# A TensorE switch around the feed-forward's low-part products, and the third norm's last step on GpSimd, in a one-core decoder layer

## The chip, the cores and the metric

The kernel runs on 1 core of a Trainium2 chip. The metric is the device time of one execution in microseconds (us); the time of a kernel is the median of several runs. Engines are named as in the profile: PE is TensorE's matrix products (PEld its weight loads), DVE is VectorE, ACT is ScalarE, POOL is GpSimd, SP is the engine whose queue issues nearly all DMAs.

## What is computed

One decoder layer over 4 sequences of 1024 tokens with 512 features, float32. Cut to what matters here:

```python
x = layernorm(x + attention(x))                   # 16 features a head, 32 heads
x = layernorm(x + gated_convolution(x, ctx))      # sigmoid, tanh gates, kernel size 2
x = layernorm(x + feed_forward(x))

def feed_forward(x, ternary_weight, bias, act_scale):
    scale = maximum(act_scale, 1e-05)
    x_int = clip(round(x / scale), -127, 127)
    w = ternary_weight.astype(float32) - 1.0      # ternary_weight is drawn from 0, 1, 2
    return einsum('bsi,oi->bso', x_int * scale, w) + bias
```

So the weight of the feed-forward holds only -1, 0 and 1 for these inputs. The kernel does not rely on that: it splits the weight into a part that TensorE's `float32r` format holds (the high part) and the rest (the low part), and multiplies by both.

## The kernel before

The kernel has two halves. `attention` takes about 1700 us of the span. `tail` does the rest twice, once for the batches 0 and 2 and once for 1 and 3, with these stages:

* The second time only: the output projection `project_out` (16 tiles of 128 tokens each for a pair of batches, PE line 292).
* The gate stage: 4 times 2 times 4 gates. One gate is 32 products of 128x171 on PE (line 1205, tiles `pc` then `pa`), four DVE instructions that read them (lines 1209 to 1215) and one activation on ACT (line 1216). `pc` and `pa` have two buffers each, so PE can be two gates ahead of DVE. `combine` (lines 1231 to 1260) finishes a group of 4 gates on POOL, ACT and DVE, with the second norm.
* The feed-forward, `feed_forward`: 16 tiles of 128 tokens. For a tile, `quantise` scales on ACT (line 1281) and clips on POOL, or on DVE for the first tiles (line 1282); `turn` transposes on PE (line 1288, four products) and ACT copies the result to `xq_t` (line 1290); `feed` multiplies on PE (line 1298); `residual` is two DVE instructions (lines 1303 and 1304). The third norm follows in groups of four tiles: mean and variance on DVE (line 1314), a root on ACT (line 138), inversion and shift on DVE (lines 139 and 1321), and last the step `finish` per tile, on ACT where its number is even (line 1332) and on DVE where it is odd (line 142), and a DMA of the tile to the output by SP (line 1337). The very last tile is done in two halves of 256 columns.

`feed` has 8 products for a tile: the four 128-row parts of the high weight `w_hi`, then the four parts of the low weight `w_lo`, all into one PSUM tile:

```python
        for n, w in enumerate((hand.w_hi, hand.w_lo)):
            for f in range(FT):
                last = n == 1 and f == FT - 1
                nc.tensor.matmul(pt, xq_ts[b, t][:, f, :], w[:, f, cols], start=n == f == 0, stop=last)
```

Both weights are made during the first gate stage by `halves_of_w_f`: for each of the four parts a cast (line 255) and a subtraction (line 256) on POOL, and a DMA that writes the difference to DRAM (line 257); last a DMA reads the whole low weight back as `w_lo` (line 261).

The order of the work is written out by hand. `step()` is called after every gate and every tile, and counts; `after(n, work)` runs a piece of work n steps later, so it stands on its engines' queues behind the instructions of that gate or tile. The pieces of `halves_of_w_f` are put at steps 17, 19, 21, 23 and 25 of the first gate stage, which has 32 steps. Each engine executes its own queue in order, and a wait at its head holds everything behind it.

Of the kernel before, what the change touches and what calls it, by code (L numbers as in the profile page):

```python
# [8 lines left out]
F32 = mybir.dt.float32  # L9
F32R = mybir.dt.float32r  # L10
AF = mybir.ActivationFunctionType
ALU = mybir.AluOpType
AX = mybir.AxisListType
PSUM = bass.MemoryType.PSUM

P = 128
B, S, D = 4, 1024, 512
NH, HD = 32, 16
NG = 8
FT = D // P  # L20
# [9 lines left out]
@with_exitstack  # L30
def decoder_kernel(ctx: ExitStack, tc: tile.TileContext, a, out):
    nc = tc.nc

    outer = ctx.enter_context(tc.tile_pool(name="outer", bufs=1))
    ident = outer.tile([P, P], F32, tag="ident", name="ident")
    make_identity(nc, ident)
    eps = outer.tile([P, 1], F32, tag="eps", name="eps")
    nc.gpsimd.memset(eps, EPS)

    dram = ctx.enter_context(tc.tile_pool(name="dram", bufs=1, space=bass.MemoryType.DRAM))
    attn_d = [dram.tile([D, S], F32, tag=f"attn{b}", name=f"attn{b}") for b in range(B)]


    shared = ctx.enter_context(tc.tile_pool(name="shared", bufs=1))
    hand = Handed(tc, a, shared, attn_d, eps)
    with ExitStack() as attn:
        attention(attn, tc, a, attn_d, ident, shared, hand)
    with ExitStack() as rest:  # L50
        tail(rest, tc, a, out, ident, eps, hand, dram)
# [11 lines left out]
class Handed:  # L63
# [74 lines left out]
        nc.scalar.activation(part, mv[:, t0 : t0 + n, 1], AF.Sqrt, bias=self.eps, scale=1.0)  # L138
        return rstd, lambda: nc.vector.reciprocal(part, part)

    def normalised(self, dst, src, mv, rstd, t):
        self.nc.vector.tensor_scalar(
            dst, src, mv[:, t, 0:1], rstd[:, t : t + 1], ALU.subtract, ALU.mult
        )

# [98 lines left out]
        w = self.w_f[:, f, :]  # L244
        self.nc.gpsimd.tensor_scalar_add(w, w.bitcast(mybir.dt.int32), -1.0)

    def halves_of_w_f(self, pool, dram):


        nc, w = self.nc, self.w_f  # L250
        self.w_hi = pool.tile([P, FT, D], F32R, tag="w_hi", name="w_hi")
        low_d = dram.tile([P, FT, D], F32, tag="w_low", name="w_low_d")

        def part(f):
            nc.gpsimd.tensor_copy(self.w_hi[:, f, :], w[:, f, :])
            nc.gpsimd.tensor_sub(w[:, f, :], w[:, f, :], self.w_hi[:, f, :].bitcast(F32))
            nc.sync.dma_start(low_d[:, f, :], w[:, f, :])

        def last():
            self.w_lo = self.shared.tile([P, FT, D], F32R, tag="w_f", name="w_lo")  # L260
            nc.sync.dma_start(self.w_lo.bitcast(F32), low_d)

        return [lambda f=f: part(f) for f in range(FT)] + [last]

    def prepare_rest(self):
        nc = self.nc
# [872 lines left out]
def tail(ctx, tc, a, out, ident, eps, hand, dram):  # L1139
    nc = tc.nc  # L1140
    fir = ctx.enter_context(tc.tile_pool(name="fir", bufs=1))
    bigs = ctx.enter_context(tc.tile_pool(name="bigs", bufs=1))
# [5 lines left out]
    ps_t = ctx.enter_context(tc.tile_pool(name="ps_t", bufs=2, space=PSUM))  # L1148
# [11 lines left out]
    def after(steps, work):  # L1160
        later.append((now + max(steps, 1), work))
# [113 lines left out]
    xqs, xq_ts, stats3 = {}, {}, {}  # L1275
# [16 lines left out]

    def feed(b, t, cols=slice(0, D)):
        pt = ps_o.tile([P, D], F32, tag="o", name=f"pf{b}_{t}_{cols.start}")[:, 0 : cols.stop - cols.start]
        for n, w in enumerate((hand.w_hi, hand.w_lo)):
            for f in range(FT):
                last = n == 1 and f == FT - 1
                nc.tensor.matmul(pt, xq_ts[b, t][:, f, :], w[:, f, cols], start=n == f == 0, stop=last)  # L1298
        return pt

    def residual(b, n, t, pt, cols=slice(0, D), half=0):
# [4 lines left out]
    def third_norm(b, n0, n):  # L1306

        y = ys2[b]
        made = []

        def first():
            for m in range(n0, n0 + n):
                halves = 2 if (b, m) == (B - 1, NT - 1) else 1
                nc.vector.bn_aggr(mv3[b][:, m, :], stats3[b][:, m : m + halves, :].rearrange("p h c -> p (h c)"))
            made.extend(hand.deviations(mv3[b], stat, f"3_{b}", n0, n))

        def invert():
            made[1]()
            shift = stat.tile([P, NT], F32, tag="shift", bufs=4, name=f"shift{b}_{n0}")
            part = slice(n0, n0 + n)  # L1320
            nc.vector.scalar_tensor_tensor(
                shift[:, part], mv3[b][:, part, 0], -1.0, made[0][:, part], ALU.mult, ALU.mult
            )
            made.append(shift)

        def finish(m):
            t = order[m]
            n = 2 if (b, m) == (B - 1, NT - 1) else 1
            for h in range(n):
                part = y[:, t, h * D // n : (h + 1) * D // n]  # L1330
                if m % 2 == 0 or h == 1:
                    nc.scalar.activation(
                        part, part, AF.Identity, bias=made[2][:, m : m + 1], scale=made[0][:, m : m + 1]
                    )
                else:
                    hand.normalised(part, part, mv3[b], made[0], m)
                (nc.scalar if h else nc.sync).dma_start(
                    out[b, t * P : (t + 1) * P, h * D // n : (h + 1) * D // n], part
                )

        return first, invert, [lambda m=m: finish(m) for m in range(n0, n0 + n)]


    order = [t // 2 + t % 2 * 4 for t in range(NT)]
    mv3 = {}

    def feed_forward(batches):
# [6 lines left out]
        for k, (b, n, t) in enumerate(tiles):  # L1354
# [3 lines left out]
            if (b, n) == (B - 1, NT - 1):  # L1358

                for half in range(2):  # L1360
                    cols = slice(half * 256, half * 256 + 256)
                    pt = feed(b, t, cols)
                    residual(b, n, t, pt, cols, half)

                    for work in closing:
                        work()
                    closing = []
            else:
                pt = feed(b, t)
                if k + 3 < len(tiles):  # L1370
                    quantise(tiles[k + 3][0], tiles[k + 3][2], nc.vector if k < 3 else nc.gpsimd)

                while roots:
                    roots.pop()()
                if n >= 6:
                    for work in closing:
                        work()
                    closing = []
                residual(b, n, t, pt)
# [29 lines left out]
    after(5, lambda: hand.load_attention(1, big1))  # L1409
    for m, work in enumerate(scaling):  # L1410
        after(9 + m, work)
    for m, work in enumerate(hand.halves_of_w_f(bigs, dram)):
        after(17 + 2 * m, work)

    k = 0
    for n, batches in enumerate(((0, 2), (1, 3))):
# [11 lines left out]
        for t in range(4):  # L1428
            w = w_next
# [65 lines left out]
```

## Time and profile before

| what | value |
|---|---|
| median of 3 runs (lowest, highest) | 2144.36 us (2143.28, 2148.23) |
| the profiled execution's own time | 2147.72 us |
| its span, first to last instruction | 2145.8 us |
| mean granted TensorE clock | 0.998 |
| PE busy in the span | 2109.5 us (98%) |
| DVE / ACT / POOL busy | 1728.0 / 1388.3 / 977.5 us |
| first feed-forward, first product to the start of the projection | 1854.97 to 1894.92 us |
| second feed-forward, first product to the end of the last | 2099.97 to 2140.12 us |

How to read it: times inside the execution count from the first instruction of the span. A row of the timeline has start, duration, engine, line, operation, output and inputs, shapes and count, and in square brackets the idle time before it with what ended that. An engine that is busy all the time sets the pace of its stage only if the others wait for it. The 1.9 us between the span and the execution's own time lie around the span.

### The profile page before, as it was taken

The numbers are of one execution on the slowest core, as the hardware profiler recorded it, in microseconds if no ns is written. First come the engines' busy times: TensorE is split into PE (matmuls) and PEld (weight loads), VectorE is DVE, ScalarE is ACT, GpSimd is POOL, SyncE is SP. The second block draws the span as 40 slices with busy tenths as digits, with TensorE's granted clock in tenths as the row PEclk, the third lists the DMA queues.
The fourth block names the chain that finished last, engine by engine and source line by source line (L and its number), as shares of the span: only waits on it lengthen the run. The fifth ranks groups of instructions, "written<-read, shape, count | busy, mean of one in ns | idle before, by whom it ended". The sixth has DMA issues, their size and how long they took to land.

```text
span 2145.8 us, 81983 instructions
## 1 busy us (share of the span) xinstructions
PE 2109.5 (98%) x35404; PEld 1528.9 (71%) x35404; DVE 1728.0 (81%) x3068; ACT 1388.3 (65%) x2771; POOL 977.5 (46%) x1298
## 2 busy tenths in 40 slices
PE   9999999999999999999999999999999999999998
PEld 6666666666666666666666666667766799858997
DVE  3678888888888888888888888888897566779667
ACT  1157777777777777777777777777777623521336
POOL 2562534333344334343533333645464369532773
PEclk9999999999999999999999999999999999999999
DMA  7513213332322233122313124422411243270222
GB/s 274 176 52 98 78 50 92 106 123 64 102 54 78 63 103 107 60 88 88 106 54 111 54 75 132 147 64 84 123 47 52 60 163 118 74 279 21 100 78 79
DMA packets 114538, 207.97 MB, mean 97 GB/s; under 512 B 36992, under 2 KB 37248, under 8 KB 114048
## 3 DMA queue, kind: packets, MB, share of 16 engines
q1 hardware_dynamic: 113456, 201.55, 29.4%
q8 instruction: 277, 4.54, 0.9%
q10 hardware_dynamic: 720, 1.18, 0.2%
q14 instruction: 85, 0.70, 0.1%
HBM read 132.41 MB, written 69.73 MB: 94 GB/s over the span
## 4 chain that ended last, share of the span: by engine, by line
PE 84%; DVE 13%; POOL 1%; issue 1%; ACT 1%; DMA 0%; SPq 0%; DVEq 0%; ACTq 0%; POOLq 0%
PE av L872 23%; PE nat L758 15%; PE st L835 10%; DVE mx L771 9%; PE part L60 9%; PE pa L1205 6%; PE pc L1205 6%; PE v L60 5%; PE po L60 3%; PE po L292 3%; PE fold L425 1%; PE proj L60 1%; PE pf L1298 1%; PE fold L60 1%; DVE stats L1304 1%
## 5 line engine op out<-in xcount | busy, mean ns | idle before, releaser
L771 DVE TENSOR_REDUCE mx<-nat 128x1 f32<-128x512 f32 x2048 | 1271.4, 684 | 197.8 <-PE nat L758 179.5
L844 ACT ACTIVATE at<-st 128x512 f32<-128x512 f32 x2016 | 1042.2, 603 | 320.5 <-PE st L835 316.6
L758 PE MATMUL nat<-qk 32*128 32x512 f32 x4096 | 712.1, 421 | 2.2 <-DVE v_sb L658 1.3
L835 PE MATMUL st<-qk 32*128 32x256 f32 x8064 | 681.7, 290 | 0.2
L835 PEld LDWEIGHTS st<-qk 32*128 32x128 f32 x8064 | 526.1, 184 | 4.9 <-issue 2.1
L835 PE MATMUL st<-qk,ones 2*128 2x256 f32 x4032 | 504.1, 287 | 0.0
L872 PE MATMUL av<-at,v_sb 128*32 128x256 f32 x8192 | 499.4, 382 | 4.2 <-ACT at L844 1.3
L758 PEld LDWEIGHTS nat<-qk 32*128 32x128 f32 x4096 | 328.6, 184 | 203.0 <-DVE mx L771 162.6
L872 PEld LDWEIGHTS av<-at,v_sb 128*32 128x32 f32 x8192 | 240.8, 109 | 182.3 <-DVE mx L771 25.2
L835 PEld LDWEIGHTS st<-qk,ones 2*128 2x128 f32 x4032 | 353.6, 183 | 0.0
L1216 ACT ACTIVATE u<-u,b_c 128x512 f32<-128x512 f32 x64 | 46.2, 723 | 159.6 <-DVE u L1215 155.7
L778 POOL CAST neg<-least 128x16 fp32r<-128x16 f32 x64 | 12.7, 199 | 216.0 <-DVE least L776 216.0
L885 DVE TENSOR_TENSOR o_sb<-av,o_sb 128x256 f32<-128x256 f32 x128 | 54.4, 425 | 61.6 <-PE av L872 61.2
L722 POOL TENSOR_TENSOR y<-y,extra 128x256 f32<-128x256 f32 (+8 forms) x152 | 73.5, 518 | 65.9 <-ACT extra L708 65.9
L1212 DVE SCALAR_TENSOR_TENSOR u<-pa,u 128x342 f32<-128x342 f32 x64 | 40.6, 634 | 67.5 <-PE pa L1205 66.3
L921 POOL TENSOR_TENSOR o_n<-o_sb,o_n 128x512 f32<-128x512 f32 x64 | 83.3, 1324 | 13.3 <-DVE u L1213 13.3
L450 POOL TENSOR_TENSOR extra<-extra,highs 128x512 f32<-128x512 f32 x62 | 79.6, 1284 | 5.0
L1205 PE MATMUL pa<-xf,w 128*128 128x171 f32 x512 | 80.4, 308 | 0.5 <-POOL w L196 0.5
L1205 PE MATMUL pc<-xf,w 128*128 128x171 f32 x512 | 79.8, 308 | 0.0
L883 ACT COPY o_sb<-av 128x256 f32<-128x256 f32 x128 | 48.1, 376 | 46.9 <-PE av L872 36.7
L1205 PEld LDWEIGHTS pa<-xf,w 128*128 128x128 f32 x512 | 76.0, 189 | 1.0 <-POOL w L196 1.0
L1205 PEld LDWEIGHTS pc<-xf,w 128*128 128x128 f32 x512 | 76.0, 189 | 0.0
(210 smaller groups left out, 2782.3 us busy)
## 6 DMA issues: line engine op xcount, KB each, us to landing
qk<-qk_d SPq DMA_DIRECT2D x96, 512.0 KB
qk_d<-highs SPq DMA_DIRECT2D x96, 256.0 KB
qk_d<-extra SPq DMA_DIRECT2D x96, 256.0 KB
u<-in_ctx SPq DMA_DIRECT2D x16, 1024.0 KB
xT<-in_xT SPq DMA_DIRECT2D x16, 512.0 KB
o_n<-rec_d SPq DMA_DIRECT2D x128, 64.0 KB
attn<-o_n SPq DMA_DIRECT2D x256, 32.0 KB
y<-in_x SPq DMA_DIRECT2D x16, 512.0 KB
```

The source lines that it names most:

```text
L60: nc.tensor.matmul(pt[r, :], lhsT(f)[:, r], rhs(f), start=f == 0, stop=f == tiles - 1)
L292: nc.tensor.matmul(pt, attn_t[:, f, t * P : (t + 1) * P], self.w_o[:, f, :], start=f == 0, stop=f == FT - 1)
L450: eng.tensor_sub(block, block, high)
L722: eng.tensor_add(c, c, x)
L758: lambda n=n, r=r, turn=turn: nc.tensor.matmul(pts[n], qk_sets[u % 3][turn][r : r + 32, qt * P : (qt + 1) * P], qk_sets[u % 3][2][r : r + ...
L771: nc.vector.tensor_reduce(mxs[u][:, qt, j, kh : kh + 1], pts[n], AX.X, ALU.max, negate=True)
L835: lambda st=st, k=k, n=n, left=left, right=right: nc.tensor.matmul(st[:, k * QW : k * QW + QW], left, right, start=n == 0, stop=n == 2),
L844: nc.scalar.activation(at, st, AF.Exp, scale=0.25)
L872: nc.tensor.matmul(av[32 * j : 32 * j + 32, :], v_sb[b % 2][:, kt, c * VW : c * VW + 32], ats[u, 2 * i + n // 2, j][:, n % 2 * QW : n % 2 ...
L885: nc.vector.tensor_add(o, av, o)
L921: nc.gpsimd.tensor_mul(part, o_sb[:, cols].rearrange("p (s e) -> p e s", e=2), part)
L1205: nc.tensor.matmul(pt, w[i][:, tap, o : o + P], xf[:, tap, i, :], start=i == 0, stop=i == FT - 1)
```

## The change

Three things are changed.

1. In `halves_of_w_f`, two DVE reductions per part take the largest value and the negated smallest value of the low weight. A new piece `compare`, at step 27, reduces these 8 columns to one, multiplies it on PE by a column of positive constants (which adds up the 128 rows), and compares the sum with zero on DVE into a one-word tile `flag`. A new piece `read`, at step 29, loads `flag` into a register of PE.
2. `feed` issues three high products, and then a `Switch` of PE on that register with two arms. Arm 0 has the last high product. Arm 1 has the last high product and the four low ones. There are 33 such places (31 tiles, and one tile in two halves).
3. `finish` of the third norm goes to POOL, but for the last four tiles of batch 3, which stay as they are.

```diff
-    def normalised(self, dst, src, mv, rstd, t):
-        self.nc.vector.tensor_scalar(
+    def normalised(self, dst, src, mv, rstd, t, eng=None):
+        (eng or self.nc.vector).tensor_scalar(
...
+        lows = self.shared.tile([P, 2 * FT + 1], F32, tag="lows", name="lows")
+        flag = self.shared.tile([1, 1], mybir.dt.int32, tag="flag", name="flag")
...
             nc.sync.dma_start(low_d[:, f, :], w[:, f, :])
+            nc.vector.tensor_reduce(lows[:, f : f + 1], w[:, f, :], AX.X, ALU.max)
+            nc.vector.tensor_reduce(lows[:, FT + f : FT + f + 1], w[:, f, :], AX.X, ALU.min, negate=True)
+
+        def compare():
+            top = lows[:, 2 * FT : 2 * FT + 1]
+            nc.vector.tensor_reduce(top, lows[:, 0 : 2 * FT], AX.X, ALU.max)
+            pt = ps.tile([P, FT, P], F32, tag="t", name="any_low")[0:1, 0, 0:1]
+            nc.tensor.matmul(pt, top, self.magic, start=True, stop=True)
+            nc.vector.tensor_scalar(flag, pt, 0.0, None, ALU.is_gt)
+
+        def read():
+            engine = mybir.EngineType.PE
+            why = "a comparison gives nought or one"
+            self.any_low = {
+                engine: nc.values_load(
+                    flag, engines=[engine], min_val=0, max_val=1, skip_runtime_bounds_check_because=why
+                )
+            }
...
-        return [lambda f=f: part(f) for f in range(FT)] + [last]
+        return [lambda f=f: part(f) for f in range(FT)] + [last, compare, read]
...
     def feed(b, t, cols=slice(0, D)):
         pt = ps_o.tile([P, D], F32, tag="o", name=f"pf{b}_{t}_{cols.start}")[:, 0 : cols.stop - cols.start]
-        for n, w in enumerate((hand.w_hi, hand.w_lo)):
-            for f in range(FT):
-                last = n == 1 and f == FT - 1
-                nc.tensor.matmul(pt, xq_ts[b, t][:, f, :], w[:, f, cols], start=n == f == 0, stop=last)
+        def product(w, f, start=False, stop=False):
+            nc.tensor.matmul(pt, xq_ts[b, t][:, f, :], w[:, f, cols], start=start, stop=stop)
+
+        for f in range(FT - 1):
+            product(hand.w_hi, f, start=f == 0)
+        for arm in tc.Switch(hand.any_low, n=2):
+            product(hand.w_hi, FT - 1, stop=arm == 0)
+            if arm:
+                for f in range(FT):
+                    product(hand.w_lo, f, stop=f == FT - 1)
         return pt
...
-                if m % 2 == 0 or h == 1:
+                if b != B - 1 or m < 4:
+                    hand.normalised(part, part, mv3[b], made[0], m, nc.gpsimd)
+                elif m % 2 == 0 or h == 1:
...
-    for m, work in enumerate(hand.halves_of_w_f(bigs, dram)):
+    for m, work in enumerate(hand.halves_of_w_f(bigs, dram, ps_t)):
         after(17 + 2 * m, work)
```

In the order in which the changed program issues its instructions on PE, one `feed` reads: three products; `SwitchStride`; two register instructions; then arm 0, which is a branch prefetch hint, one product and an unconditional branch; then arm 1, which is a hint, five products and an unconditional branch; then the next tile's transposes.

More of the change, by code (lines that the diff above doesn't have):

```diff
@@ L245, in prepare_w_f, with halves_of_w_f @@
         self.nc.gpsimd.tensor_scalar_add(w, w.bitcast(mybir.dt.int32), -1.0)
-    def halves_of_w_f(self, pool, dram):
+    def halves_of_w_f(self, pool, dram, ps):
         nc, w = self.nc, self.w_f
+        lows = self.shared.tile([P, 2 * FT + 1], F32, tag="lows", name="lows")
+        flag = self.shared.tile([1, 1], mybir.dt.int32, tag="flag", name="flag")
         self.w_hi = pool.tile([P, FT, D], F32R, tag="w_hi", name="w_hi")
```

## The prediction

> **What bounds the kernel now.** I read the page's busy times first, then the timeline of PE in a feed-forward, then the DMA queues of the page, because the change adds branches and PE's code comes by DMA.
>
> ```profile
> PE 2109.5 (98%) x35404; PEld 1528.9 (71%) x35404; DVE 1728.0 (81%) x3068; ACT 1388.3 (65%) x2771; POOL 977.5 (46%) x1298
> ...
> q8 instruction: 277, 4.54, 0.9%
> ```
>
> PE is busy 98% of the span, so time that PE loses or saves is lost or saved at the end. The change touches two feed-forwards: PE's first product to the projection's start is 1854.97 to 1894.92 (39.95 us), and the second, to the end of its last product, 2099.97 to 2140.12 (40.15 us). In their steady part one tile looks like this:
>
> ```profile
> 1870.82 0.60 PE L1288 MATMUL tr<-ident,xq 128*128 128x128 f32 x4
> 1871.18 1.16 PE L1298 MATMUL pf<-w_hi,xq_t 128*128 128x512 f32 x4
> 1872.18 1.09 PE L1298 MATMUL pf<-w_lo,xq_t 128*128 128x512 f32 x4
> 1873.11 0.60 PE L1288 MATMUL tr<-ident,xq 128*128 128x128 f32 x4
> ```
>
> From start to start: 0.36 us of transposes, 1.00 of high products, 0.93 of low products, 2.29 a tile, with no idle time. PE sets the pace; the others need less per tile: DVE 0.75 + 0.69 (lines 1303, 1304) + some 0.24 for the means and roots = 1.68 without `finish`, ACT 0.69 + 0.80 + 0.08 = 1.57, POOL 0.62.
>
> **What goes.** The weight is -1, 0 or 1, which the cast of line 255 holds exactly, so the low part and the flag are zero and arm 0 runs: 132 low products, 0.93 us a tile, 30 us of PE in all. If branches were free, the pace would fall to DVE's 1.68.
>
> **What the switch costs.** No row of before shows a computed jump, so I bound it. From below: PE, DVE, ACT and POOL each pass one unconditional branch at the program's start, and in the timeline's first microsecond POOL's instructions before and behind it (0.34 + 0.10 to 0.73) are 0.29 us apart. That is a jump to code that is already there.
>
> From above: a jump to code that isn't. Queue q8 shows how PE's code arrives. Its 277 packets carry 4.54 MB, 16.4 KB each; PE and PEld have 35404 instructions each, 70808 / 277 = 256 a packet. So PE's code is streamed in blocks of 256 instructions, and a packet takes 0.009 x 16 x 2145.8 / 277 = 1.12 us on its DMA engine. Straight code hides this, since a block lasts 2145.8 / 277 = 7.7 us. A jump out of the loaded blocks can't hide it. The nearest row for a whole round trip is the 16 KB transfer of line 793 and the wait of SP's next instruction for its landing:
>
> ```profile
> L793 SPq DMA_DIRECT2D rows_d<-turned x64: 527/542/607, 103.7 to 1660.6; - x64
> ```
>
> ```profile
> SPq L798 <- DMA rows_d<-turned: 80.1, 46, 5.9
> ```
>
> The issue takes 0.54 us, the wait behind it 80.1 / 46 = 1.74. That transfer is cut over many DMA engines, a code block is one packet on one; I add its 1.12. One block fetch F is then estimated at 0.54 + 1.74 + 1.12 = 3.4 us; its ends are 1.12 (the packet alone) and 4.5 (a second packet, of the next block in line, ahead of it).
>
> Are the arms out of the loaded blocks? In the changed program's order a `SwitchStride` stands before the jump: arm n lies n strides behind arm 0. Each arm opens with a prefetch hint for the branch that ends it. I read a hint as a sign that the target is in a block that isn't there yet. Both speak for arms in blocks of their own, with the code behind them in one more. I take this as likeliest. Then the tile's chain on PE's sequencer is: enter the block behind the last switch, whose following block (the next arm 0) is called for now; run about 1.4 us of transposes and three products; wait till F is over; enter the arm, whose hint calls for the block behind; its one product ends at once; wait a second F. A tile takes 2F = 6.8 us in place of 2.29, and PE, DVE, ACT and POOL all fit into it.
>
> * First feed-forward: the first arm has been called for long before; its exit costs F, 15 more tiles 2F each: 31 x 3.4 = 105.4 against 39.95, **+65.5**.
> * Second: 17 switches, and the last tile's result needs no exit: 32 x 3.4 + 0.64 (the last products) = 109.4 against 40.15, **+69.3**.
>
> [...]
>
> **Flag.** The eight reductions of 128x512 are priced at 0.68 each (line 771's row), 1.37 a part, on DVE in the gate stage, which PE paces at 4.67 us a gate. They stand behind POOL's subtraction, and everything DVE owes the next gates stands behind them. The tightest is the first: POOL's subtraction (line 256) starts at 1788.51 and takes 1.28, so the reductions end at 1791.2 and the next `pc` is read by 1791.85. PE needs that buffer at 1792.51: hidden, by 0.65 us.
>
> `compare` is not hidden. PE's product waits for DVE's reduction, and all gates stand behind it. It comes after the 27th gate:
>
> ```profile
> 1828.55 2.50 PE L1205 MATMUL pa<-xf,w 128*128 128x171 f32 x16
> ...
> 1834.04 0.86 DVE L1215 SCALAR_TENSOR_TENSOR u<-pa,u 128x513 f32<-128x513 f32 x1
> ```
>
> PE is done at 1831.05; DVE, late by a clip and two `bn_stats`, ends that gate at 1834.9, and with the small reduction PE goes on at about 1835.2: **+4.2**. An idle PE also loses clock. After 1.89 us of idle at 1721.89 the windows' table has (PEclk is the last column but two):
>
> ```profile
> 1723.00:1727.00 4.00, 4.00 (x18) 4.00 (x17) 1.78 (x4) 0.72 (x1) 2.75 (x3) 0.57 0.98 387
> ```
>
> 0.43 x 4 = 1.7 us lost. I count it twice where PE must be quick again, after `compare` and at the projection: **+3.4** (ends 0 and 3.4). The load of the flag into PE's register lies between 0 (PE's queue still has products) and the 2.3 us of the round trip above; I take **+1**.
>
> **Third norm on POOL.** 28 tiles lose 0.81 us on ACT or 0.53 on DVE. POOL's price is not shown with column operands; between its clip (0.64, line 1282) and a tensor-tensor (1.25, line 1260). I take 0.64, the nearest in form. At 6.8 us a tile it costs nothing; at a pace of 1.7 POOL would need 1.3 to 1.9 a tile, and at 1.9 be the bound. SP's DMAs of the output wait for POOL instead, with the loads of the next stage behind them, which have the projection's 55 us. Batch 3's last four tiles, and so the end of the program, are unchanged.
>
> **Sum.** 65.5 + 69.3 + 4.2 + 3.4 + 1 = 143.4. The profiled execution's 2147.72 becomes 2291.1; against the median, 2144.4 + 143.4 = **2288**.
>
> **Rivals.**
>
> * *One fetch a switch is exposed* (arm 0's block is already there, or the hint comes in time). A tile is F + 1.4 = 4.8: first stage 15 x 4.8 + 3.4 = 75.4 (+35.5), second 16 x 4.8 + 0.64 = 77.4 (+37.3), with the 8.6 of flag and clock +81: 2226. For it: the hint exists. Against: one product after the hint gives it no time.
> * *The code is there* (several blocks loaded ahead, or arms in one block): the other side. The switch is then 0.3 us or less, hidden, and DVE's 1.68 sets the pace: 0.6 us x some 22 steady tiles = 13, less 4.2 + 1.7 + 1 = 6.9 (one clock dip), about -6: 2138, or 2131 if `compare` is hidden too. It decides from 63F + 0.6 + 8.6 = 80.1 on, F = 1.13: a fetch must cost less than a packet alone. For it: nothing in the trace excludes deeper loading. Against: the hints, and one packet per block all along.
> * *F is near its low end of 1.12*: 2.24 a tile is the old pace; no change, 2144.
> * *The flag is not zero* and arm 1 runs: its four low products hide under the fetches; 2288 or a few us above.
>
> **Chances.** Two fetches 0.55, one fetch 0.25, code there 0.13, F small 0.04, flag set 0.03. So faster by over 0.2% 0.13, within 0.2% (about what a measurement of this kernel can tell from no change) 0.04, slower 0.83. Within the likeliest case F from 2.3 (the round trip with no packet added) to 4.5 gives 63 x 2.3 + 0.6 - 80.1 + 8.6 = +74 to +213. The range 2212 to 2350 takes in nearly all of that and the one-fetch case, and leaves out the 17% that end near or below today's time.
>
> **What would show it.** Right: in the feed-forwards PE idles twice a tile with "issue" or nothing as its releaser, tiles 5 to 9 us apart; q8 has two to three more packets per switch, 66 to 99 in all; no `w_lo` products; ACT and DVE wait for PE. Wrong: tiles 1.7 to 2.3 apart with DVE waiting for nothing, q8 near 277, or POOL between PE's tiles.

## The result, and the profile after

The changed kernel takes 2342.53 us (2339.84 to 2343.96) against 2144.94 (2143.28 to 2148.23): 1.0918 times the time before, 95% interval 1.0899 to 1.0937, 197.6 us more. The forecast was 2288 in a range of 2212 to 2350. Its span is 2338.1 us against 2145.8, with a mean granted clock of 0.942 against 0.998.

The page after, the lines that answer to those of before:

```profile
PE 2130.6 (91%) x35274; PEld 1526.1 (65%) x35274; DVE 1723.3 (74%) x3064; ACT 1379.6 (59%) x2757; POOL 1034.8 (44%) x1326
...
PEclk9999999999999999999999999999999955999855
...
q8 instruction: 374, 6.13, 1.2%
...
PE 77%; DVE 12%; issue 6%; POOL 3%; ACT 1%; POOLq 0%; DMA 0%; SPq 0%; DVEq 0%; ACTq 0%
```

PE executes 130 products fewer on balance (132 low ones less, and two rows for the comparison) and yet is idle for 9% of the span. "issue" is now 6% of the chain that ended last: time in which PE waited for nothing that the profile shows. PE's code queue q8 brought 97 blocks more, 2.9 for each of the 33 switches. And the granted clock is near half in the two feed-forwards: 0.54 and 0.51 over 40 us of each.

The steady tile, in PE's weight loads of the second feed-forward (start, duration, engine, line, operation, tiles, shape, count, idle time before):

```profile
2222.43 0.72 PEld L1310 LDWEIGHTS tr<-ident,xq 128*128 128x128 f32 x4 [4.69 <-issue]
2223.13 0.98 PEld L1318 LDWEIGHTS pf<-w_hi,xq_t 128*128 128x128 f32 x3
2225.81 0.29 PEld L1318 LDWEIGHTS pf<-w_hi,xq_t 128*128 128x128 f32 x1 [1.70 <-issue]
2230.52 0.72 PEld L1310 LDWEIGHTS tr<-ident,xq 128*128 128x128 f32 x4 [4.42 <-issue]
```

The transposes are the first work behind the last switch, the single product is the arm. From the transposes to the arm 3.38 us, from the arm to the next transposes 4.71, together 8.09 where a tile took 2.29. Over 14 tiles of this stage the means are 3.29 and 4.84. Both ends of a tile wait for "issue"; no engine is what PE waits for. What it waits for has rows of its own, on the queues (count, then shortest, median and longest in ns):

```profile
L1521 PEldq COMPARE_BRANCH  x66: 343/4553/6207, 1857.9 to 2331.8; - x66
L1521 ACTq COMPARE_BRANCH  x33: 33/33/38, 1857.2 to 2313.4; - x33
```

PE has two branches a switch. The one into the arm takes 2.4 to 3.1 us in 28 of 33 switches, the one out of it 4.5 to 5.3 in 32. The very first branch into an arm, while no packet is under way, takes 0.34. The other four engines pass 33 branches each that the kernel before doesn't have, of 32 to 53 ns.

PE's branches and q8's packets at the same place, from the trace's records (start and duration in us):

```
branch into the arm     2222.85 2.81                    |   2230.94 2.57
  packet                2223.35 0.96                    |   2231.12 0.88
branch out of the arm   2225.90 4.57                    |   2233.69 4.98
  packets               2226.41 1.19 and 2226.90 2.17   |   2234.20 2.01 and 2234.68 1.97
```

One packet starts 0.6 to 0.9 us after the transposes begin (2222.43, 2230.52), and the branch into the arm ends 1.4 to 1.5 us after that packet (2224.31, then 2225.66; 2232.00, then 2233.51). Two packets start 0.5 and 1.0 us after the branch out of the arm does. One or both of the two take about 2 us in place of 0.9 to 1.2, and the branch ends 1.4 us after the second in the first tile (2229.07, then 2230.47) and 2.0 us after it in the next (2236.65, then 2238.67). Which of the two brings the target is not shown.

Where the 192.3 us between the two profiled spans are, from the starts of the first product, of the projection and the end of the last product:

| part | before | after | more |
|---|---|---|---|
| up to the first feed-forward | 1854.97 | 1859.69 | 4.7 |
| first feed-forward, to the projection | 39.95 | 135.71 | 95.8 |
| projection and gates, to the second | 205.05 | 206.83 | 1.8 |
| second feed-forward, to the end of its last product | 40.15 | 130.1 | 89.9 |
| rest | 5.7 | 5.8 | 0.1 |

The first row hides something. From the gate stage's first product with the tile `w` (1741.18 before, 1737.12 after) to the first feed-forward it is 113.8 us before and 122.6 after: 8.8 more, less 4.1 us by which this execution came earlier to that point. With 8.8 in place of 4.7 the rows add up to 196.4, and the medians are 197.6 apart.

### The profile page after: what moved, and what is told of

It reads as the page before. It is cut to its first block, busy times and chain, and to the rows that moved or that the text cites. A ratio compares the mean times of both kernels' runs of the same rounds, so it can differ in the third digit from the quotient of the medians.

```text
span 2338.1 us, 82062 instructions
## 1 busy us (share of the span) xinstructions
PE 2130.6 (91%) x35274; PEld 1526.1 (65%) x35274; DVE 1723.3 (74%) x3064; ACT 1379.6 (59%) x2757; POOL 1034.8 (44%) x1326
## 4 chain that ended last, share of the span: by engine, by line
PE 77%; DVE 12%; issue 6%; POOL 3%; ACT 1%; POOLq 0%; DMA 0%; SPq 0%; DVEq 0%; ACTq 0%
PE av L894 21%; PE nat L780 14%; PE st L857 9%; PE part L60 9%; DVE mx L793 8%; PE pc L1227 5%; PE pa L1227 5%; PE v L60 4%; PE po L314 2%; PE po L60 2%; POOL y L142 2%; PE tr L1310 1%; PE pf L1318 1%; PE fold L447 1%; PE proj L60 1%
## 5 line engine op out<-in xcount | busy, mean ns | idle before, releaser
L1331 DVE SCALAR_TENSOR_TENSOR y<-pf,sc,big 128x512 f32<-128x512 f32 (+1 forms) x33 | 24.2, 734 | 182.7 <-PE pf L1318 174.8
L1310 PE MATMUL tr<-ident,xq 128*128 128x128 f32 x128 | 32.3, 404 | 112.2 <-issue 103.8
L1318 PE MATMUL pf<-w_hi,xq_t 128*128 128x512 f32 (+1 forms) x132 | 74.5, 666 | 54.5 <-issue 54.5
L1312 ACT ACTIVATE xq_t<-tr,unmagic 128x512 fp32r<-128x512 f32 x32 | 21.8, 686 | 165.9 <-PE tr L1310 165.9
L1310 PEld LDWEIGHTS tr<-ident,xq 128*128 128x128 f32 x128 | 21.3, 203 | 126.1 <-issue 116.7
L1318 PEld LDWEIGHTS pf<-w_hi,xq_t 128*128 128x128 f32 x132 | 36.6, 308 | 79.5 <-issue 76.6
```

Of the source, the lines that this page charges most:

```text
L1310: nc.tensor.transpose(tr[:, f, :], xqs[b, t][:, f * P : (f + 1) * P], ident)
```

## The experiments

The theory: a switch costs two waits for code, one to enter the arm and one to leave it, because the arms and the code behind them lie in blocks of their own; a wait is set by how many packets are called for and when. The rivals: PE's own work at half clock; GpSimd's step, which takes 2.08 us where 0.64 was priced; the flag; and a jump that costs the same wherever it leads.

**e_free: the change with a switch that costs nothing.** It leaves out the low products.

```diff
-        for f in range(FT - 1):
-            product(hand.w_hi, f, start=f == 0)
-        for arm in tc.Switch(hand.any_low, n=2):
-            product(hand.w_hi, FT - 1, stop=arm == 0)
-            if arm:
-                for f in range(FT):
-                    product(hand.w_lo, f, stop=f == FT - 1)
+        for f in range(FT):
+            product(hand.w_hi, f, start=f == 0, stop=f == FT - 1)
```

> The change without its switch: flag, register load and GpSimd's step stay, the four low products are left out (they are zero here), so this is the change with a switch that costs nothing. The prediction's rival said DVE's 1.68 us would set the pace, 2138. The theory after the result: the switch's code fetches are nearly all of the +198, so this falls to near the old time; but GpSimd's step took 2.08 us in the changed kernel, with its clip 2.7 a tile, above TensorE's old 2.29, so I expect 2150 to 2165 and not 2138. If the switch were not the cause, it would stay above 2250.

Measured: 2177.13, ratio 1.0145 (1.0131 to 1.0159), 276 packets in q8. So 165 of the 198 us go when the switch goes. But the rest is no small thing, and more than I expected: with free branches the change would still have been 32 us slower. What holds it is mostly on POOL: PE's transposes wait 23.1 us in all for its clip, and PE 7.2 in the projection and 4.1 for the flag.

```profile
1881.14 0.61 POOL L1304 TENSOR_SCALAR xq<-xq 128x512 f32<-128x512 f32 x1
...
1881.81 0.66 PE L1310 MATMUL tr<-ident,xq 128*128 128x128 f32 x4 [2.71 <-POOL xq L1304]
1881.86 2.08 POOL L142 TENSOR_SCALAR y<-y,mv,rstd 128x512 f32<-128x512 f32 x1
...
1884.01 0.61 POOL L1304 TENSOR_SCALAR xq<-xq 128x512 f32<-128x512 f32 x1
```

The clip that PE's transposes wait for stands behind the last step of the norm, once a tile: 2.08 + 0.61 and the gaps are 2.87 us a tile.

**e_norm: GpSimd's step alone.** All eight products, no flag, no switch; `finish` as in the change.

> The third norm's step on GpSimd alone: no flag, no switch, all eight products. The prediction priced GpSimd's step at 0.64 us and would say no change (2144 to 2146). With 2.08 + 0.62 = 2.7 us a tile on GpSimd against TensorE's 2.29 and some 24 such tiles in the loops: 0.4 x 24 = 10, so 2150 to 2160. Both are far from +198.

Measured: 2166.89, ratio 1.0099 (1.0085 to 1.0112), 22 us more. The direction was right, the size twice what I expected. I had counted the loops only. The queues behind POOL cost as well: at the end of the first stage nine steps stand on POOL in a row, SP's output DMAs wait for them, and the load of the next stage's tokens waits behind those:

```profile
1892.08 18.52 POOL L142 TENSOR_SCALAR y<-y,mv,rstd 128x512 f32<-128x512 f32 x9
```

```profile
1907.20 0.69 DVE L316 TENSOR_TENSOR y<-y,b_o 128x512 f32<-128x512 f32 x1 [7.80 <-DMA y<-in_x]
```

```profile
1908.75 3.75 PE L312 MATMUL po<-w_o,big 128*128 128x512 f32 x4 [5.49 <-DVE y L317]
```

SP issues that load at 1902.90, 6.7 us after the projection's start (1896.23); before it did so at 1894.65, 0.3 us ahead of it. DVE waits for it, PSUM is not read, and PE stands for 5.5 us in the projection. At the end of the program five such steps run from 2149.60 to 2159.90, past the last tile's own end.

**e_flag: the flag alone.** All eight products, third norm as before; nothing uses the register.

> The flag alone: the reductions, the comparison and the register load are made, nothing uses the register, all eight products, third norm as before. Prediction: 4.2 of wait + 1.7 of clock + 1 of register load, 2151 to 2152. From the changed kernel's trace: 4.1 us of idle TensorE and about 3 us of the half clock behind it, the register load hidden, 2151 to 2152 as well. If the flag hides, 2145.

Measured: 2154.6, ratio 1.0043 (1.0029 to 1.0056), 9.4 us more by the medians, above the 2151 to 2152 that were expected. From the first product with `w` to the first feed-forward it is 122.4 us (1737.94 to 1860.35) where before it is 113.8: 8.6 more. PE in that run:

```profile
1809.13 1.14 PE L1227 MATMUL pc<-xf,qk_w 128*128 128x171 f32 x6 [1.04 <-DVE u L1231]
...
1826.67 2.49 PE L1227 MATMUL pa<-xf,w 128*128 128x171 f32 x16
1833.27 0.19 PE L269 MATMUL any_low<-magic,lows 128*1 128x1 f32 x2 [4.11 <-DVE lows L267]
1833.39 4.93 PE L1227 MATMUL pc<-xf,w 128*128 128x171 f32 x16
1838.11 2.98 PE L1227 MATMUL pa<-xf,w 128*128 128x171 f32 x16
```

The reductions are not quite hidden: once, behind the third part's (DVE has them from 1807.27 to 1808.55), PE waits 1.04 us for a buffer. For `compare` it waits 4.11 us, then needs 4.93 and 2.98 us for what takes 2.50 each: 2.9 us for the clock. That makes 8.0 of the 8.6; the rest stays open. The load of the flag into the register takes 0.49 us in the changed kernel's trace and nobody waits for it.

**e_nolow: the high products alone.** No low products, no flag, no switch; third norm as before.

> The high products alone: the four low ones are left out (zero here), no flag, no switch, third norm as before. TensorE then needs 1.36 us a tile; DVE with its share of the last step 1.95 and ACT 1.97 set the pace: 0.3 us x about 24 steady tiles = 7 us faster, 2136 to 2139. If the pace of the feed-forward is set by a round trip of quantise, turn and copy and not by TensorE, nothing is gained, 2145.

Measured: 2142.29, ratio 0.9985 (0.9976 to 0.9994): faster, by 3 us and not 7. It is the only version that beats both kernels, and only because the low part is left out. PE's 30 us go, and what is late next takes nearly all of it:

```profile
1876.72 1.19 PE L1316 MATMUL pf<-w_hi,xq_t 128*128 128x512 f32 x4 [0.75 <-ACT xq_t L1310]
1878.13 0.66 PE L1308 MATMUL tr<-ident,xq 128*128 128x128 f32 x4 [0.22 <-POOL xq L1302]
1879.56 1.20 PE L1316 MATMUL pf<-w_hi,xq_t 128*128 128x512 f32 x4 [0.78 <-DVE rstd L139]
1881.11 0.66 PE L1308 MATMUL tr<-ident,xq 128*128 128x128 f32 x4 [0.34 <-POOL xq L1302]
```

PE now waits in turn for the copy to `xq_t`, for the clip and, by the profile's guess, for DVE (the reciprocal that it names is no input of the products). That part of the old pace was PE's by a small margin only.

**e_switch: the change without GpSimd's step.** `finish` as before, flag and switch stay.

> The changed kernel with the third norm's last step put back on ACT and DVE; flag and switch stay. If two code fetches a switch set the pace of 8.1 us a tile, GpSimd's 2.7 us are hidden and this is within 3 us of the changed kernel, 2339 to 2343. If GpSimd's 2.08 us step is on the path (the trace names it as the releaser of some transposes), 2320 or less.

Measured: 2341.95, ratio 1.0915 (1.0889 to 1.0942): the same as the changed kernel. At 8.1 us a tile POOL's 2.7 are hidden, and so the 22 us of e_norm do not show in the change at all. Without GpSimd's step the switch therefore costs more than the 165 us of e_free: e_nolow's 2142.29 with e_flag's 9.4 is 2151.7, 190 us under this run (an estimate from three runs).

**e_fill: four more products a tile, ahead of the switch.** All high products and three low ones stand in front; both arms hold the last low product.

```diff
-        for f in range(FT - 1):
-            product(hand.w_hi, f, start=f == 0)
+        for f in range(FT):
+            product(hand.w_hi, f, start=f == 0)
+        for f in range(FT - 1):
+            product(hand.w_lo, f)
         for arm in tc.Switch(hand.any_low, n=2):
-            product(hand.w_hi, FT - 1, stop=arm == 0)
...
+            product(hand.w_lo, FT - 1, stop=True)
```

> The three last high products and the first three low ones stand ahead of the switch, and both arms hold only the last low product: four more products a tile are executed than in the changed kernel. Theory (code fetches set the pace): they fit into the 3 us in which the next arm is fetched, even at half clock (4 x 0.5), so 2335 to 2350. Rival (TensorE's own work at half clock sets the distance from one switch to the next): 4 x 0.33 to 0.4 more a tile, +45 to +55, 2390 or so.

Measured: 2343.78, ratio 1.0932 (1.0914 to 1.095): 132 products more for nothing. The granted clock over 40 us of it was 0.70 against 0.54 in the changed kernel, and that did not help either. PE's work and its clock do not set the distance between switches in this kernel.

**e_three: four arms in place of two.** `n=4`, arms 1 to 3 alike.

> Four arms in place of two (the register is still 0, arms 1 to 3 are alike and not taken). Theory: at the arm's entry the next block in line and the hinted block behind the arms are fetched, the blocks between are not; three packets a switch as with two arms, 2340 to 2346. Rival (all blocks that are jumped over are fetched in line): five packets a switch, 33 x 2 x about 1 us more, 2400 or more.

Measured: 2340.54, ratio 1.0914 (1.0896 to 1.0932), 373 packets. Five packets a switch would have made some 440 (276 and 33 x 5). At 2.9 packets a switch, as with two arms, the two arms more brought no packets of their own.

**e_swap: the last arm is taken.** The comparison is `is_ge`, so the flag is 1, and the arms are exchanged.

> The comparison is turned so that the flag is 1, and the arms are exchanged, so the same products are executed by the last arm in place of the first. Theory: what a jump costs follows from where its target lies. The exit's target is now the very next block, called for by one packet on entry of the arm: about 3.2 us in place of 4.9. The arm's target is now two blocks on and not called for until the jump: with the packet of arm 0's block still under way it rises from 3.2 to 4.5 to 6 us. Together 2325 to 2375, with the two parts visibly exchanged. Rival (the exit is the dear jump because of what it is, the branch behind a hint): exit stays at 4.9.

Measured: 2353.27, ratio 1.0973 (1.0954 to 1.0991), 374 packets. PE's weight loads:

```profile
1889.70 0.71 PEld L1310 LDWEIGHTS tr<-ident,xq 128*128 128x128 f32 x4 [2.76 <-DVE mv L1342]
1890.40 0.97 PEld L1318 LDWEIGHTS pf<-w_hi,xq_t 128*128 128x128 f32 x3
1894.90 0.29 PEld L1318 LDWEIGHTS pf<-w_hi,xq_t 128*128 128x128 f32 x1 [3.53 <-issue]
1897.90 0.71 PEld L1310 LDWEIGHTS tr<-ident,xq 128*128 128x128 f32 x4 [2.71 <-issue]
```

Now it is 5.20 us to the arm and 3.00 to the exit (means over 13 tiles of the second stage 5.16 and 3.17), the two parts exchanged. The trace's records show the same exchange: the branch into the arm takes 4.3 to 4.8 us in 28 of 33 switches and has two packets, the one out of it 2.8 to 3.5 in 32 of 33 and has one. What a jump cost here followed from where its target lies in the program's order: 3.0 to 3.3 us where it is next in line and one packet was under way, 4.8 to 5.2 where it is a block further and two packets were. (The releaser in the first line's brackets is a guess of the profile: DVE's means are not an input of the transposes.)

**e_pair: one switch for two tiles.** `feed` takes two tiles, and the arm ends both; the last two tiles of a stage stay single, and the very last has two halves: 19 switches, not the 18 that the expectation counts.

> One switch for two tiles (14 tiles of each stage in pairs; the last two tiles of a stage singly, the last one of all in halves): 18 switches in place of 33, with the same products, flag and GpSimd step as in the changed kernel. Theory: a switch costs about 8.1 us whatever is done between two of them, as long as that stays under it, so 15 x 8.1 = 121 us less, 2215 to 2230. If the cost belonged to the tiles (half clock, GpSimd's 2.08 us, waits between engines), well less than half would go, 2290 or more.

Measured: 2244.96, ratio 1.0464 (1.0447 to 1.0482), 333 packets, 57 more than e_free's and 3.0 for each of 19 switches. 98 us less for 14 switches, 7.0 each and not 8.1. Per switch the direction holds; the size does not, because the work between two switches is no longer hidden: with two tiles in a row PE waits for the copies of the pair.

```profile
1887.05 1.09 PE L1310 MATMUL tr<-ident,xq 128*128 128x128 f32 x8 [2.43 <-issue]
1888.55 0.79 PE L1324 MATMUL pf<-w_hi,xq_t 128*128 128x512 f32 x1 [0.40 <-ACT xq_t L1312]
1889.83 3.35 PE L1324 MATMUL pf<-w_hi,xq_t 128*128 128x512 f32 x7 [0.49 <-ACT xq_t L1312]
...
1895.72 1.97 PE L1310 MATMUL tr<-ident,xq 128*128 128x128 f32 x8 [2.54 <-issue]
```

```profile
L1533 PEldq COMPARE_BRANCH  x38: 312/4192/7245, 1858.5 to 2236.0; - x38
```

This pair takes 8.7 us where two tiles took 16.2. What is hidden now is the way into the arm: its packet starts at 1887.72, 0.7 us after the pair's transposes, and ends at 1888.76, and the branch comes only at 1890.10 and takes 0.40. Of the 19 branches into an arm 12 take 0.31 to 0.42 us, near the 0.34 of the changed kernel's very first one; I read that as the price of a jump to a block that is there. So that packet goes with entering the block and not with the branch. The branch out of the arm is not helped: 4.6 to 5.2 us in 18 of 19.

**e_onearm: a switch with one arm.** This one told nothing new.

> The switch has one arm only (the arm with the four low products is left out), all else as in the changed kernel. Theory: the code behind the arm is then the very next block, so entering the arm calls for one packet and not two that share a DMA engine; the exit falls from 4.9 us to about 3.2, 1.6 x 33 = 53 us less, 2285 to 2295, and two packets a switch in place of three (about 341 in all). If a jump costs the same wherever its target lies, 2340.

Measured: 2177.3, ratio 1.0152 (1.0135 to 1.0169), 276 packets, and no branch in the trace: a switch of one arm is straight code, and the kernel is e_free once more (2177.13). e_swap asks the same question with two arms.

## Why the prediction was right or wrong

**Two fetches a switch: right in kind, the exit mis-sized.** The likeliest case of the forecast (0.55) is the one that came. It had one F of 3.4 for both, 6.8 a tile. Entering the arm measured 3.29, the exit 4.84, together 8.13. The term that was too small is the second F, "enter the arm, whose hint calls for the block behind; ... wait a second F": two packets go out there and not one, and together they take longer (one or both 1.7 to 2.4 us at 32 of the 33 exits, where a packet alone takes 0.9 to 1.3 in most cases). That they are the hinted block and the next in line is argued, not shown; e_swap and e_three agree with it. I had such a pair as F's upper end (4.5), for both fetches. With 31 entries at 3.29 and 32 exits at 4.84 in place of 63 x 3.4, the two stages come to 257.5 with the last products, less 80.1 = 177.4; forecast were 134.8, measured 185.7. The other 8 us are in single longer distances of the first stage: 4.64, 5.99 and 5.63 us to three arms, 6.38 from one. There a packet starts late: 1.7 to 3.1 us after the branch into the arm, the second one 3.8 us after the branch out of it. The 5.99 stands out at the same tile in e_switch (5.91), e_three (5.66) and e_swap (7.88), so it goes with the place in the code; that a tile's straight code runs over a block's end there is a guess that was not tried.

**Where the miss lies.** Of the 54 us by which the rise was above the forecast (197.6 against 143.4), 51 are in the two feed-forwards and 2 at the flag.

**A jump to loaded code.** The row for the lower bound of 0.29 was misread: between POOL's two instructions the trace has a drain of 0.19 us and two semaphore instructions, and no branch. The price was near all the same, by luck: 0.31 to 0.42 us in e_pair, 0.34 for the first switch.

**The arms' blocks.** Taken from the program's order (a stride, a hint in each arm). q8's 374 packets against 277 and e_swap's exchanged waits agree with it. The changed kernel's trace has 33 hints, of 35 to 50 ns; what a hint calls for has no row. That a jump out of the loaded blocks can't hide its fetch held at all 33 exits (4.5 to 5.3 us at 32 of them, 6.2 at one).

**The estimate from a data transfer.** 0.54 + 1.74 + 1.12 = 3.4 was near the 3.0 to 3.3 of a single fetch, but its parts are others: some 0.7 till the packet starts, 0.9 to 1.2 of packet, 1.4 behind it. The trace of before has the transfer as 128 packets of 128 bytes, of 13 ns each in the median, up to 7 at a time, and a code block as one packet of 16384; over how many DMA engines they go has no row. That the sums nearly meet is luck.

**Flag.** Forecast 4.2 + 1.7 + 1 = 6.9, measured 8.6 to 8.8 in the gate stage. The wait was 4.1, the clock 2.9 and not 1.7, the register load hidden. The reductions, put at nothing because the first part's would hide, cost one wait of 1.0 us at the third part.

**Third norm on GpSimd: hidden, as forecast, but the price was wrong.** Between 0.64 and 1.25 was the bound; it took 2.08, outside of it. The row nearest in form was not near: the clip has constants, this step has two columns of 128 values as operands. It changed nothing here (e_switch), and it would have decided the rival.

**The rival on the other side.** "The code is there: 2138." e_free is that case without its switch, and it took 2177. Two reasons: the price on POOL, and the queues behind it, which the prediction named and covered with "the projection's 55 us"; in e_norm the load of tokens, behind the outputs on SP, came 7 us later against the projection's start and PE stood for 5.5. Even with GpSimd left as it was and no flag, e_nolow gains only 3 us.

**Clock at the projection.** Forecast 1.7, measured 1.8: the projection took 56.8 us in place of 54.9, with a granted clock of 0.78 over its first 8 us.

## What to carry to other kernels

In this kernel a branch on PE was priced by where its target lay: the two jumps of a switch took 3.29 and 4.84 us in the mean of the second feed-forward, against 0.93 us for the products that the switch skips. For such a change, count the engine's code blocks from the code queue's packets, and price each jump out of the loaded ones from a trace with a switch in it. The wait was hidden where enough work stood between entering a block and the jump to the next, as at 12 of e_pair's 19 arms (0.31 to 0.42 us). A low-cost test of such a change is to leave the branch out and keep its gain: e_nolow shows that in this order of the work there were some 3 us to win. A step that is moved to another engine needs a row of the same form of operands there (2.08 us where 0.64 was priced), and everything that stands behind it on that queue and on the DMA queue counts (22 us in e_norm, 10 expected).

## What the runs showed of the hardware

* A code packet of 16 KB for PE, in the changed kernel's feed-forwards: alone it took 0.9 to 1.3 us in most cases; of two that ran together one or both took 1.7 to 2.4. With a packet alone the jump went on 1.3 to 1.6 us after its end.
* With a target next in the program's order, a jump cost 3.0 to 3.4 us in most tiles, from the first weight load of one block to that of the next (3.29 in the mean at the changed kernel's arms, in the second feed-forward); with the target further on, 4.8 to 5.2 (4.84 at its exits); the branch took 0.40 us where the packet had ended 1.3 us before it (the pair shown of e_pair), and 0.31 to 0.42 at 12 of the 19 arms of that run.
* PE's branches took 0.34 us and more in the changed kernel and 0.31 and more in e_pair; those of the other four engines, in the changed kernel, 32 to 53 ns.
* GpSimd's subtract-and-multiply of 128x512 float32 with two columns as operands took 2.08 us, its clip of the same shape with two constants 0.61; VectorE's median for the former was 0.55.
* After 4.1 us of idle PE (e_flag) two groups of 16 products took 4.93 and 2.98 us in place of 2.50 each, 2.9 more; after 4.14 us in the changed kernel the granted clock was 0.62 over the next 7.7 us.
